# A mixer's input projection as 2x2 block products with seven multiplications

## The chip, the core and the metric

The kernel runs on one core of a Trainium2 chip. A core has a matrix engine (TensorE, "PE" in the profile; the loading of its stationary operand is listed apart as "PEld"), a vector engine (VectorE, "DVE"), an engine for functions of one argument (ScalarE, "ACT"), a general one (GpSimd, "POOL") and one that starts transfers (SyncE, "SP"). Each takes its own list of instructions in order, and they wait for each other by semaphores. [...]

The metric is the device time of one execution in microseconds: the median of three runs is 2827.87 us (2827.24 to 2828.50).

## What is computed

Three stages on 512 tokens (8 sequences of 64) of 512 numbers, all in float32: a cross attention, a state-space mixer, and a routed low-rank layer, each added to its input. The change is in the mixer:

```python
proj = einsum('bld,pd->blp', hidden_states, in_proj_w)   # hidden: the normed x
gate = proj[..., :I]                                     # I = 4096
hbc = proj[..., I:I + CONV_DIM]                          # CONV_DIM = 6144
dt = proj[..., -H:]                                      # H = 64 heads
pad = pad(hbc, ((0, 0), (K - 1, 0), (0, 0)))             # K = 4 taps
conv = conv_bias
for k in range(K):
    conv = conv + pad[:, k:k + L, :] * conv_weight[:, k]
xBC = silu(conv)                  # x (4096), B (8 x 128), C (8 x 128)
dt_p = softplus(dt + dt_bias)
dA = exp(dt_p * -exp(A_log))
# scan over tokens: state = state * dA + (dt_p * x) B^T;  y = state C
y = y + x * D
yn = (yg * rsqrt(var + EPS)).reshape(B, L, I) * norm_weight   # var per group of 512
yn = yn * silu(gate)
out = einsum('bli,di->bld', yn, out_proj_w)
```

## The kernel before, in words

The mixer (`mixer_and_routed`) works on eight groups, each of ten blocks of 128 rows of `in_proj_w`: four gate blocks (n = 0 to 3), four x blocks (4 to 7), B (8) and C (9). Its input `xnT` holds the normed tokens, transposed: 128 partitions by four chunks (`dc`) by 512 tokens.

`project(G, n)` (L1101 to L1127) makes one block: four matmuls into a PSUM bank "pj" (L1105), of which there are three, shared with the output projection "mo". A gate block is finished by one Silu on ACT (L1111). For the others DVE reads the bank four times: first tap and bias (L1116), then three taps added with a shift by one to three tokens (L1122), and ACT applies Silu (L1127).

Per 128 tokens (`tt`, four of them) there are further steps: `mix` (products of B and C, transposes of x into "px", and on DVE the tiles gm, m and dx: L1143 to L1156), `scan` (32 small matmuls into two banks, added to y by DVE: L1172, L1178), `squares` (ACT and POOL: L1184 to L1187), `gate` (DVE: y times silu(gate), L1194), `norm` (the factor rs, with Ln and Exp on ACT: L1200 to L1204) and `project_out` (L1213, added to x by DVE in L1217). `decay` makes the exponentials of the scan (matmuls L1093, Exp on ACT L1098) from tiles `av` that POOL makes (`steps`, L1078). `skip` puts x * D into y on POOL (L1134), and `load_out` scales `w_out` by the norm's weights on POOL (L1004).

The groups are pipelined by hand in the loop at L1275 and on. In the first half of a turn the new group's convolution blocks (8, 9, 4 to 7) alternate with the older group's mix, scan and gate. Then ACT changes its table from Silu to Ln and Exp, does the next group's decays and the older group's norm, and changes back; in the second half the new group's four gate blocks alternate with the older group's four output products. `tc.issue_after(ins)` keeps what its block traces on the engine of `ins` behind `ins` in that engine's list; all these uses name an instruction of ACT. Within such bounds a scheduler sets the lists when the program is built.

The first group has no older one. It is preceded by the layer norm, the dt product (`pdt`), and a chain on DVE and ACT (L1024 to L1045) that makes softplus, `dt` and `a`; from `a` come `psw` (a matmul, L1054), `ah`, `av` and the decays, behind which ACT's first Silus are put.

The block products that the change uses are in the kernel already, for the queries, keys and values of the attention: `FIRST` and `SECOND` (L38, L39) list seven products of half-size blocks, `weight_sums` (L137 to L145) makes the four sums of weights on POOL with 128x256 additions. In the queries (`project_queries`, L149 to L235) a pair's `first` step ends with sums on DVE (p1 copied by ACT at L220, then u2 at L222, t at L224), and the `second` step of the pair before runs between; banks "ab" and "cd" exist three times each.

Of the kernel before, what the change touches and what calls it, by code (L numbers as in the profile page):

```python
# [47 lines left out]
DT0 = I2 + CONV  # L48

# [901 lines left out]
def mixer_and_routed(ctx, tc, c, x, done, w_in, w_out, w_ra, b_w, out):  # L951
# [43 lines left out]
    def load_out(G):  # L995

        g = G.g
        G.wo = wst.tile([P, GC, D], F32, tag="w_out", name=f"w_out_{g}")
        nc.sync.dma_start(
            out=G.wo, in_=w_out[g * GC * P : (g + 1) * GC * P, :].rearrange("(n p) o -> p n o", p=P)  # L1000
        )
        for n in range(GC):
            ct = g * GC + n
            nc.gpsimd.tensor_scalar(G.wo[:, n, :], G.wo[:, n, :], c.nw[:, ct : ct + 1], None, op0=ALU.mult)  # L1004

    load_in(groups[0])

# [13 lines left out]

    dt = big.tile([P, NTT, H2], F32, name="dt")
    z = big.tile([P, NTT, H2], F32, name="sp_z")
    nc.vector.tensor_tensor(z, pdt, c.dtb.unsqueeze(1).to_broadcast([P, NTT, H2]), ALU.add)  # L1024
    e = big.tile([P, NTT, H2], F32, name="sp_e")
# [4 lines left out]
    u = big.tile([P, NTT, H2], F32, name="sp_u")  # L1030
    nc.vector.tensor_scalar(u, e, 1.0, None, op0=ALU.add)
    lu = big.tile([P, NTT, H2], F32, name="sp_lu")
# [68 lines left out]
    def project(G, n):  # L1101

        pj = bank("pj", [P, NT], "pj", 3)
        for dc in range(DC):
            nc.tensor.matmul(  # L1105
                pj, lhsT=G.w[:, dc, n, :], rhs=xnT[:, dc, :], start=dc == 0, stop=dc == DC - 1
            )
        if n < GC:
            if n == 0:
                G.sg = grpp.tile([P, GC, NT], F32, tag="sg", name="sg")  # L1110
            return nc.scalar.activation(G.sg[:, n, :], pj, AF.Silu).ins  # L1111
        if n == 8:
            G.xbc = grpp.tile([P, GC + 2, NT], F32, tag="xbc", name="xbc")
        ct = G.g * GC + n - GC if n < 8 else (I2 // P + G.g if n == 8 else I2 // P + G2 + G.g)
        acc = wk.tile([P, NT], F32, tag="acc", name="acc", bufs=3)
        nc.vector.tensor_scalar(  # L1116
            acc, pj, c.cw[:, ct, KC - 1 : KC], c.cb[:, ct : ct + 1], op0=ALU.mult, op1=ALU.add
        )
        accb = acc.rearrange("p (b t) -> p b t", b=B)
        pjb = pj.rearrange("p (b t) -> p b t", b=B)  # L1120
        for k in range(1, KC):
            nc.vector.scalar_tensor_tensor(  # L1122
                out=accb[:, :, k:], in0=pjb[:, :, : S - k],
                scalar=c.cw[:, ct, KC - 1 - k : KC - k], in1=accb[:, :, k:],
                op0=ALU.mult, op1=ALU.add,
            )
        return nc.scalar.activation(G.xbc[:, n - GC, :], acc, AF.Silu).ins  # L1127

    def skip(G):

        G.y = grpp.tile([P, GC, NT], F32, tag="y", name="y")
        for n in range(GC):
            ct = G.g * GC + n
            nc.gpsimd.tensor_scalar(G.y[:, n, :], G.xbc[:, n, :], c.dk[:, ct : ct + 1], None, op0=ALU.mult)  # L1134
# [99 lines left out]
    def route(tt):  # L1234
        xnT = wk.tile([P, DC, P], F32, tag="xnT", name="rt_xnT")
# [28 lines left out]
        o = wk.tile([P, D], F32, tag="o", name="o")  # L1264
# [10 lines left out]
    for g in range(G2):  # L1275
# [10 lines left out]
        with tc.issue_after(last):  # L1286

            for n, behind in (
                (None, ((mix, 0),)),
                (8, ((mix, 1),)),  # L1290
                (9, ((scan, 0),)),
                (4, ((mix, 2), (scan, 1))),
                (5, ((gate, 0), (mix, 3), (scan, 2))),
                (6, ((gate, 1), (scan, 3))),
                (7, ((gate, 2), (gate, 3))),
            ):
                if n is not None:
                    silus.append(project(G, n))
                if old:
                    for what, tt in behind:  # L1300
                        what(old, tt)
# [3 lines left out]
        with tc.issue_after(table):  # L1305
            if new:
                decay(new, 0)
                decay(new, 1)
        gates = [lambda n=n: project(G, n) for n in range(GC)]
        if new:  # L1310
# [104 lines left out]
```

## Time and profile before

| | us |
|---|---|
| median of three runs | 2827.87 |
| the profiled run | 2826.02 |
| its span, first to last instruction | 2824.3 |
| first group of the mixer, from its first projection matmul to the next group's | 2328.7 to 2372.8 (44.1) |
| one of the middle groups | 2432.1 to 2491.5 (59.4) |
| last group, to the older group's last output product | 2728.6 to 2791.1 (62.5) |

Times inside the span count from its start. A line of the table of groups of instructions names the source line, engine, operation, the written and the read tiles, shapes and count, then the busy time in us and the mean of one instruction in ns, then the idle time of the engine just before them and what ended it. A line of a timeline has the start, the duration, the engine, the source line, the operation and, in brackets, the idle time before it with what ended it. [...] A view of stretches gives the busy time of each engine in chosen parts of the span, with the granted TensorE clock (1.00 is full).

### The profile page before, as it was taken

The page shows a single profiled execution, that of the slowest core. Times are in us where ns is not written, and L with a number is a line of the kernel's source. Part 1 is how long each engine was busy: PE and PEld are TensorE (multiplying, and loading weights), DVE is VectorE, ACT ScalarE, POOL GpSimd, SP SyncE. Part 2 cuts the span into 40 slices and gives each one's busy share as a digit, 9 for nine tenths or more (in the row PEclk, how much of TensorE's full clock was granted, in tenths as well). Part 3 has the DMA queues.
Part 4 walks back from the last instruction along what each step waited for, and adds up shares of the span by engine and source line. Part 5 has one row for each costly group of instructions (what it writes and reads, how often), then busy time and mean ns, then how long its engine had stood idle before and what let it go on. Part 6 is the DMA issues. An engine that isn't in the chain of part 4 may idle for free.

```text
span 2824.3 us, 38454 instructions
## 1 busy us (share of the span) xinstructions
PE 2788.6 (99%) x14972; PEld 1980.9 (70%) x14972; DVE 1745.4 (62%) x3059; ACT 726.6 (26%) x1314; POOL 833.9 (30%) x786
## 2 busy tenths in 40 slices
PE   9899999999999999999999999999999999999998
PEld 7677777777777777777777777777777554444444
DVE  4556676676667666665666676667665416444555
ACT  3322223222222222232222222222222103222222
POOL 4323223222222332223222222322232223433431
PEclk9999999999999999999999999999999999999999
DMA  4822232232113122312311131122212441112200
GB/s 164 276 78 57 76 74 53 53 94 53 46 46 97 46 54 79 74 48 58 94 50 50 46 95 47 46 83 76 48 46 72 146 160 38 53 53 78 79 16 15
DMA packets 277230, 206.02 MB, mean 73 GB/s; under 512 B 155676, under 2 KB 240538, under 8 KB 276026
## 3 DMA queue, kind: packets, MB, share of 16 engines
q1 hardware_dynamic: 277050, 203.57, 25.2%
q8 instruction: 119, 1.95, 0.3%
q14 instruction: 61, 0.50, 0.1%
HBM read 180.87 MB, written 22.66 MB: 72 GB/s over the span
## 4 chain that ended last, share of the span: by engine, by line
PE 83%; DVE 6%; DMA 2%; ACT 1%; issue 0%; POOL 0%; SPq 0%; ACTq 0%; DVEq 0%
PE pav L596 12%; PE psc L526 11%; PE pj L1105 8%; PE pv_a L445 6%; PE pv_b L445 6%; PE pv_c L445 5%; PE pk_a L385 5%; PE pk_b L385 5%; PE pk_c L385 5%; PE mo L1213 4%; PE pv_d L445 3%; PE pk_d L385 2%; PE psn L414 2%; DMA nbs<-max_d 2%; DVE attn L574 1%; PE pvl L468 1%
## 5 line engine op out<-in xcount | busy, mean ns | idle before, releaser
L531 DVE SCALAR_TENSOR_TENSOR attn<-psc,rk,mask_sb 128x256 f32<-128x256 f32 (+1 forms) x832 | 363.4, 473 | 190.5 <-PE psc L526 188.1
L580 POOL TENSOR_TENSOR sm<-attn 128x512 f32<-128x512 f32 x64 | 82.0, 1281 | 1147.6 <-ACT attn L578 1147.6
L596 PE MATMUL pav<-attn,v 128*128 128x256 f32 (+1 forms) x1664 | 384.3, 381 | 0.0
L526 PE MATMUL psc<-q,kT 128*128 128x256 f32 x1536 | 371.5, 381 | 0.0
L596 PEld LDWEIGHTS pav<-attn,v 128*128 128x128 f32 (+1 forms) x1664 | 311.1, 190 | 55.4 <-issue 9.6
L583 POOL TENSOR_TENSOR sm<-sm,attn 128x512 f32<-128x512 f32 x256 | 339.8, 1328 | 29.4 <-DVE attn L574 10.6
L526 PEld LDWEIGHTS psc<-q,kT 128*128 128x128 f32 x1536 | 286.3, 190 | 82.4 <-issue 36.0
L1105 PE MATMUL pj<-mx_xnT,w_in 128*128 128x512 f32 x640 | 296.3, 603 | 1.3 <-DVE acc L1122 1.3
L574 DVE TENSOR_TENSOR attn<-attn,nb 128x1024 f32<-128x1024 f32 x192 | 224.7, 1216 | 68.2 <-ACT nb L571 67.9
L445 PEld LDWEIGHTS pv_a<-wv,cx 128*128 128x128 f32 x1536 | 195.5, 191 | 48.2 <-issue 41.4
L578 ACT ACTIVATE attn<-attn 128x1024 f32<-128x1024 f32 x192 | 202.5, 1058 | 71.3 <-DVE attn L574 68.5
L445 PE MATMUL pv_a<-wv,cx 128*128 128x128 f32 x1536 | 212.7, 279 | 0.0
L542 DVE TENSOR_TENSOR mx<-mx,attn 128x512 f32<-128x512 f32 x256 | 209.5, 818 | 2.0
L1105 PEld LDWEIGHTS pj<-mx_xnT,w_in 128*128 128x128 f32 x640 | 115.2, 190 | 129.4 <-issue 124.7
L385 PE MATMUL pk_a<-cx,wk 128*128 128x417 f32 (+1 forms) x512 | 193.3, 500 | 0.8 <-ACT qrs L110 0.8
L396 ACT ACTIVATE ksq<-kT 128x834 f32<-128x834 f32 (+1 forms) x128 | 109.0, 871 | 159.1 <-DVE kT L377 159.1
L637 POOL TENSOR_TENSOR o<-o,f 128x512 f32<-128x512 f32 x31 | 39.4, 1272 | 306.7 <-DMA f<-sums_d 206.3
L385 PEld LDWEIGHTS pk_a<-cx,wk 128*128 128x128 f32 x512 | 97.2, 190 | 46.1 <-issue 20.8
L1217 DVE SCALAR_TENSOR_TENSOR x<-mo,rs,x 128x512 f32<-128x512 f32 x32 | 24.0, 751 | 165.1 <-PE mo L1213 110.4
L1213 PE MATMUL mo<-w_out,y 128*128 128x512 f32 x256 | 118.1, 597 | 0.0
L571 ACT COPY nb<-nbs 128x256 f32<-128x256 f32 x64 | 24.1, 376 | 324.4 <-DMA nbs<-max_d 324.4
L1122 DVE SCALAR_TENSOR_TENSOR acc<-pj,small_consts,acc 128x504 f32<-128x504 f32 (+1 forms) x144 | 103.9, 725 | 0.7
(220 smaller groups left out, 4230.8 us busy)
## 6 DMA issues: line engine op xcount, KB each, us to landing
wk<-in_wk SPq DMA_DIRECT2D x32, 512.0 KB
wv<-in_wv SPq DMA_DIRECT2D x32, 512.0 KB
w_in<-in_w_in SPq DMA_DIRECT2D x16, 1024.0 KB
wvs<-wv_s_d SPq DMA_DIRECT2D x28, 512.0 KB
wks<-wk_s_d SPq DMA_DIRECT2D x28, 512.0 KB
cx<-in_ctxT SPq DMA_DIRECT2D x16, 834.0 KB
cx<-in_ctxT SPq DMA_DIRECT2D x16, 768.0 KB
wq<-in_wq SPq DMA_DIRECT2D x16, 512.0 KB
```

The costliest lines, as they stand in the source:

```text
L385: nc.tensor.matmul(ps[:, :w], lhsT=u.wk[l][:, dc, :], rhs=u.cx.r[ch][r][:, dc, :], start=start and dc == 0, stop=dc == 1, skip_group_check ...
L396: nc.scalar.activation(sq[ch][:, :, half, :w], u.kT[:, :, half, lo:hi], AF.Square)
L445: nc.tensor.matmul(ps[:, i * HD : (i + 1) * HD], lhsT=u.cx.r[ch][r][:, dc, i * P : (i + 1) * P], rhs=u.wv[l][:, dc, :], start=start and i ...
L526: nc.tensor.matmul(ps[:rows, t - t2, :], lhsT=lhsT, rhs=qh, start=True, stop=True)
L531: nc.vector.scalar_tensor_tensor(out=s.at[:rows, t, :].rearrange("p (h q) -> p h q", h=GQ), in0=ps[:rows, t - t2, :].rearrange("p (h q) -> ...
L542: nc.vector.tensor_tensor(s.mx2, s.mx2, s.at[:, t2 : t2 + 2, :], ALU.max)
L574: nc.vector.tensor_tensor(at[:, k : k + 4, :], at[:, k : k + 4, :], nb.unsqueeze(1).to_broadcast([P, 4, 256]), ALU.add,)
L578: nc.scalar.activation(at[:, k : k + 4, :], at[:, k : k + 4, :], AF.Exp)
L583: nc.gpsimd.tensor_tensor(sm2, sm2, at[:, i : i + 2, :], ALU.add)
L596: nc.tensor.matmul(s.av[:, 0, :], lhsT=u.v[:rows, t, hh, :], rhs=s.at[:rows, t, :], start=t == 0, stop=t == NKT - 1,)
L1105: nc.tensor.matmul(pj, lhsT=G.w[:, dc, n, :], rhs=xnT[:, dc, :], start=dc == 0, stop=dc == DC - 1)
L1213: nc.tensor.matmul(po, lhsT=G.y[:, n, tt * P : (tt + 1) * P], rhs=G.wo[:, n, :], start=n == 0, stop=n == GC - 1,)
```

## The change

1. Two blocks n and n + 1 (pairs 8 and 9, 4 and 5, 6 and 7, 0 and 1, 2 and 3: `PAIRS`) are made together. The 256 rows of weights and the 512 tokens are cut in halves, and the depth of 512 too; seven products of half size replace eight. `project` returns two steps: `first` (four products of two matmuls of 256 columns, then sums) and `second` (three products, then the rest). A pair takes two of the three "pj" banks, each holding two half results.
2. POOL makes the weight sums (`sums_in`: four 128x256 additions a pair, in three buffers), DVE four differences of blocks of xnT, once.
3. ACT copies p1 and the bank's a half, DVE adds the others into the gate tile or xbc in SBUF. The convolution then reads SBUF: the first tap with bias is on ACT, the other three on DVE as before. Silu writes in place.
4. `skip` and the scaling of w_out (`weigh_out`, now after the gate blocks) go from POOL to ACT.
5. The loop's steps are redistributed between `first` and `second`. The gate tile has one buffer instead of two, and the tiles of the softplus chain lie in a buffer of y.

```diff
-        for n in range(GC):
-            ct = g * GC + n
-            nc.gpsimd.tensor_scalar(G.wo[:, n, :], G.wo[:, n, :], c.nw[:, ct : ct + 1], None, op0=ALU.mult)
+    def weigh_out(G):
+        for n in range(GC):
+            ct = G.g * GC + n
+            nc.scalar.activation(G.wo[:, n, :], G.wo[:, n, :], AF.Copy, scale=c.nw[:, ct : ct + 1])
+
+    def sums_in(G, n):
+        l = {
+            f"L{k + 1}{e + 1}": G.w[:, 2 * e : 2 * e + 2, n + k, :] for k in range(2) for e in range(2)
+        }
+        G.l = getattr(G, "l", {})
+        G.l[n] = weight_sums(nc, l, wk.tile([P, 4, 2, P], F32, tag="ws", name="ws", bufs=3))
...
+    for o, p, q in (("T1", "R12", "R11"), ("T2", "R22", "T1"), ("T3", "R22", "R12"), ("T4", "R21", "T2")):
+        nc.vector.tensor_tensor(blocks[o], blocks[p], blocks[q], ALU.subtract)
...
     def project(G, n):
-        pj = bank("pj", [P, NT], "pj", 3)
-        for dc in range(DC):
-            nc.tensor.matmul(
-                pj, lhsT=G.w[:, dc, n, :], rhs=xnT[:, dc, :], start=dc == 0, stop=dc == DC - 1
-            )
...
+        def first():
+            st.ps = {}
+            for pair in ("ab", "cd"):
+                t = bank("pj", [P, 2, HT], f"pj_{pair}", 3)
+                st.ps[pair[0]], st.ps[pair[1]] = t[:, 0, :], t[:, 1, :]
+            for k, lhs, rhs in FIRST:
+                product(k, lhs, rhs, k in "ad", False)
+            p1 = wk.tile([P, HT], F32, tag="p1", name="p1", bufs=1)
+            nc.scalar.copy(p1, st.ps["a"])
+            st.u2 = wk.tile([P, HT], F32, tag="u2", name="u2")
+            nc.vector.tensor_tensor(st.u2, p1, st.ps["d"], ALU.add)
+            t = wk.tile([P, HT], F32, tag="t", name="t", bufs=1)
+            nc.vector.tensor_tensor(t, st.u2, st.ps["b"], ALU.add)
+            nc.vector.tensor_tensor(to[:, 1, HT:], t, st.ps["c"], ALU.add)
+
+        def second():
+            for k, lhs, rhs in SECOND:
+                product(k, lhs, rhs, False, True)
+            nc.scalar.activation(to[:, 0, :HT], st.ps["a"], AF.Silu if gate else AF.Copy)
+            nc.vector.tensor_tensor(to[:, 0, HT:], st.u2, st.ps["b"], ALU.add)
+            nc.vector.tensor_tensor(to[:, 1, :HT], st.u2, st.ps["c"], ALU.add)
+            if gate:
+                nc.scalar.activation(to[:, 0, HT:], to[:, 0, HT:], AF.Silu)
+                return nc.scalar.activation(to[:, 1, :], to[:, 1, :], AF.Silu).ins
+            for k in range(2):
+                ct = G.g * GC + n + k - GC if n < 8 else I2 // P + k * G2 + G.g
+                pj = to[:, k, :]
+                acc = wk.tile([P, NT], F32, tag="acc", name="acc", bufs=3)
+                nc.scalar.activation(
+                    acc, pj, AF.Identity, bias=c.cb[:, ct : ct + 1], scale=c.cw[:, ct, KC - 1 : KC]
+                )
+                accb = acc.rearrange("p (b t) -> p b t", b=B)
+                pjb = pj.rearrange("p (b t) -> p b t", b=B)
+                for j in range(1, KC):
+                    nc.vector.scalar_tensor_tensor(
+                        out=accb[:, :, j:], in0=pjb[:, :, : S - j],
+                        scalar=c.cw[:, ct, KC - 1 - j : KC - j], in1=accb[:, :, j:],
+                        op0=ALU.mult, op1=ALU.add,
+                    )
+                last = nc.scalar.activation(pj, acc, AF.Silu)
+            return last.ins
...
-            nc.gpsimd.tensor_scalar(G.y[:, n, :], G.xbc[:, n, :], c.dk[:, ct : ct + 1], None, op0=ALU.mult)
+            nc.scalar.activation(G.y[:, n, :], G.xbc[:, n, :], AF.Copy, scale=c.dk[:, ct : ct + 1])
...
+            for k, (n, behind) in enumerate((
+                (None, ((), ((mix, 0),))),
+                (8, (((mix, 1),), ((scan, 0),))),
+                (4, (((mix, 2), (scan, 1)), ((gate, 0), (mix, 3), (scan, 2)))),
+                (6, (((gate, 1), (scan, 3)), ((gate, 2), (gate, 3)))),
+            )):
+                steps_in = project(G, n) if n is not None else (lambda: None, lambda: None)
+                for step, also in zip(steps_in, behind):
+                    silus.append(step())
+                    if old:
+                        for what, tt in also:
+                            what(old, tt)
                 if n is not None:
+                    sums_in(G, PAIRS[k + 1])
             skip(G)
...
         with tc.issue_after(last):
+            for k, n in enumerate((0, 2)):
...
+                first, second = project(G, n)
+                first()
...
+                last_gate = second()
+                if new:
+                    sums_in(new, PAIRS[k])
...
                 if old:
-                    project_out(old, n)
+                    project_out(old, 2 * k)
+                    project_out(old, 2 * k + 1)
+            weigh_out(G)
```

## The prediction

> **What bounds the kernel now.** I read the busy shares first, then three stretches of the mixer (the first group, and the two halves of one in the middle: convolution blocks, then gate blocks with the older group's output), then the costliest groups, then timelines of the places that the change touches.
>
> ```profile
> PE 2788.6 (99%) x14972; PEld 1980.9 (70%) x14972; DVE 1745.4 (62%) x3059; ACT 726.6 (26%) x1314; POOL 833.9 (30%) x786
> ```
>
> ```profile
> 2432.10:2464.00 31.90, 31.90 (x221) 15.13 (x220) 28.28 (x49) 6.27 (x10) 18.50 (x16) 1.00 0.25 88
> 2464.00:2491.50 27.50, 27.29 (x94) 11.99 (x93) 2.87 (x4) 7.99 (x17) 4.69 (x4) 1.00 0.10 34
> 2328.70:2372.80 44.10, 42.81 (x159) 16.92 (x158) 22.83 (x41) 16.18 (x33) 18.46 (x16) 1.00 0.00 1
> ```
>
> Columns: stretch, length, then PE, weight loads, DVE, ACT, POOL busy, clock, DMA. TensorE (PE) never pauses, at full clock (1.00). But in the first half DVE is busy 28.3 of 31.9 us: it is a close second bound there, and idle in the other half. A group takes 59.4 us.
>
> ```profile
> L1105 PE MATMUL pj<-mx_xnT,w_in 128*128 128x512 f32 x640 | 296.3, 603 | 1.3 <-DVE acc L1122 1.3
> ```
>
> A float32 product is two passes, so a group's 10 x 4 products are 80 passes. The chain of waits has 8 of them in 3.43 us: 0.429 each, 34.3 us a group.
>
> **PE's share of the change.** Five pairs by seven products by two halves by two passes are 140 passes of 256 columns. The query projection has exactly these:
>
> ```profile
> 101.05 1.03 PE L204 MATMUL pq_ab<-xnT,wq 128*128 128x256 f32 x4
> 101.91 1.03 PE L204 MATMUL pq_cd<-xs,wqs 128*128 128x256 f32 x4
> ```
>
> Four start 0.86 after the last four: 0.216 each, with the 0.19 us weight loads hidden. 140 x 0.216 = 30.2, so PE is spared 4.1 us a group, 33 us in eight. That is the whole gain, if PE stays fed.
>
> **DVE's share.** A pair adds five 128x256 sums at 0.42; six blocks lose the first tap (L1116, 0.807, spacing 0.73), which goes to ACT. Per group: +25 x 0.40 - 6 x 0.73, about +5.5 us, all but 4 of it in the half where DVE is nearly full. Worse, PE now waits for DVE and ACT inside each pair. The query rows show the wait:
>
> ```profile
> 104.77 0.42 DVE L222 TENSOR_TENSOR q_u<-q_p,pq_cd 128x256 f32<-128x256 f32 x1 [3.10 <-PE pq_cd L204]
> 105.23 0.42 DVE L224 TENSOR_TENSOR q_t<-q_u,pq_ab 128x256 f32<-128x256 f32 x1
> ```
>
> u2 starts when all of `first` is done, t 0.46 later; `second` may start after t, 1.0 us after `first` ends. The queries hide this behind another pair, with six PSUM banks; the mixer has three, a pair takes two, so the next pair's c/d bank is one that this pair must vacate.
>
> **The ledger of a middle group**, from the order in which the built program issues, with durations of these rows; t = 0 is pair 8's first pass. `first` 3.46, t ready: its `second` starts at 4.5 and takes 2.6. ACT copies bank a (0.37), DVE adds b and c (done 3.1 after the start of `second`), ACT does a first tap (0.63), and DVE six taps at 0.66 (end 7.35). Only then stands u2 of the next pair in DVE's queue, and t 0.9 later: 8.3 us from `second` to `second`, against 6.05 us of PE work in a pair. The older group's m, dx, y and gate products in the same queue make it 9.4 and 9.7 by my count; PE fills with its scans, transposes, half of the next pair and an output block. From the last `second` to the last silu 8.1. So the first half takes 4.5 + 9.4 + 9.7 + 8.1 = 31.7, against 31.9: DVE has become its bound, and PE's 24 us of projections, scans and transposes, with 7 us pulled forward, don't fill it.
>
> ```profile
> 2464.05 1.28 ACT L116 ACT_TABLE_LOAD   x1
> ...
> 2465.34 0.66 ACT L1098 ACTIVATE dec<-seg 128x256 f32<-128x256 f32 x2
> ...
> 2472.18 0.20 ACT L1204 ACTIVATE rs<-rs 128x4 f32<-128x4 f32 x1
> ...
> 2472.42 0.75 DVE L1217 SCALAR_TENSOR_TENSOR x<-mo,rs,x 128x512 f32<-128x512 f32 x1 [9.05 <-ACT rs L1204]
> ```
>
> Second half: today PE bridges the 8 us from the last silu to rs with 13 us of whole blocks. After the change, ACT's queue is table load 1.28, skip 0.63, eight decays, rs (7.3 after the silu), and only then p1 of gate pair 0, which its `second` needs; behind it queue four w_out scalings (2.5 us) and the silu table, ahead of the silu that empties bank a. DVE's u2 stands behind x (0.75), so t comes 9.6 after the silu. PE has 5 to 6 us for that gap (transposes, decays, sums, half an output block): it waits 3 to 4. Then gate pair 0's `second` 2.6, three output blocks less the half done (8.6), gate pair 1 (6.05) and 0.3 of waits: 27.1, against 27.5. A group is 31.7 + 27.1 = 58.8: of 4.1 us, 0.6 is left.
>
> **POOL and the port.** POOL loses eight scalings (4 x 1.77 and 4 x 1.57 = 13.3) and gains 20 weight sums of 0.73 = 14.6: level, and each sum is issued a half group before its use, so I cost their lateness at nothing; uncovered it would be 2.9 us a pair. But the 18 taps now read two SBUF tensors (PSUM and SBUF before: 0.64 to 0.74, always). Early in the trace:
>
> ```profile
> 43.95 0.75 DVE L256 SCALAR_TENSOR_TENSOR q_st<-q_raw,qw,qrsb 128x512 f32<-128x512 f32 x1 [1.66 <-DMA qrsb<-rs_d]
> ...
> 45.71 0.72 POOL L141 TENSOR_TENSOR wqs<-wq 128x256 f32<-128x256 f32 x1 [4.42 <-DMA wq<-in_wq]
> 45.73 1.25 DVE L256 SCALAR_TENSOR_TENSOR q_st<-q_raw,qw,qrsb 128x512 f32<-128x512 f32 x1
> 46.39 1.18 POOL L143 TENSOR_TENSOR wqs<-wq 128x256 f32<-128x256 f32 x1
> ```
>
> Beside a weight sum such an op takes 1.25 instead of 0.75, and the sum 1.18 instead of 0.73: +0.5 a collision. In the order, eight or nine POOL ops fall into the three tap windows. From none to all colliding: 0 to 4.4 us; I take half, 2.2, as POOL ops also fall beside the sums from PSUM. The group is then 61.0, +1.6; six middle groups +9.6 (bounds -4 to +23).
>
> [...]
>
> **The first group** has no older work to fill with.
>
> ```profile
> 2338.68 0.41 DVE L1045 SCALAR_TENSOR_TENSOR a<-dt,a_sb 128x256 f32<-128x256 f32 x1
> ```
>
> ```profile
> 2341.29 8.05 POOL L1078 TENSOR_TENSOR av<-ah,upto 128x512 f32<-128x512 f32 x8 [53.63 <-ACT ah L1062]
> ```
>
> PE runs 26 passes of projection from 2328.7 on while the softplus chain on DVE makes `a`. In the new order PE has only pair 8's a, d and b ahead of psw, which needs `a`; ACT's p1 is queued behind all eight decays, so u2 waits for the chain, av on POOL and the decays. Without the convolutions between, but with four block differences (0.65 each), `a` comes at 2338.2, av from 2339.5 at 1.04 each, the last decay at 2345, t at 2346.3: 17.7 us after the start, in which PE has 8.8 us of work. Then three loops of 8.3 less the overlap to the last silu (24.6), and 16.2 for decays and two gate pairs: 58.5 against 43.8, +14.7. Without the 8.9 us of waits ahead of t it would be +5.8; that is my lower bound.
>
> [...]
>
> **The last group** has its sums early and much filler: 62.5 us today, PE spared 4.1, about 2 given back in waits: -2. Table loads are as many as before; in-DMAs the same; SP's order changes only in where the last loads stand. The T sums and the sp tiles are in the first group's count.
>
> **Sum.** +14.7 + 9.6 - 2 = +22 us. The profiled run took 2826.02 (span 2824.3), 1.9 under the median of 2827.87; both versions carry the same frame, so 2827.87 + 22 = 2850.
>
> **Rivals.**
> - *PE stays the bound* (faster): the waits are filled better than my ledger says. Six groups at -4.1, the last at -4, the first still +12: -17, 2811. For it: PE waited 2 us a group so far, and each pair's wait is only 1 to 3 us. Against: the loop of 8.3 is longer than a pair's 6.05. It decides if DVE's extra 2 us per pair run while PE has blocks that hold no bank. 0.15.
> - *Even groups*: no collisions, only the first group pays: -4 + 14.7 - 2 = +9, 2837. 0.2, half of it with a first group near +5.8 (a sum of 0), which is within 0.2% (5.7 us, about what can be told from none).
> - *The port* (slower still): every tap collides, and the slower taps delay each loop: 65 to 66 us a group, +6 x 6.3 + 14 = +52, 2880. 0.12.
> - *The forecast*: 2850, from 2838 to 2866. 0.53.
>
> That the change would not do what it says is excluded: the built program holds 70 products of 256 columns a group and 16 of 512.
>
> Chances: faster 0.15, same 0.1, slower 0.75. The range leaves out the far half of the first rival and of the port case: 2815 to 2875.
>
> **What would show it.** Passes of pj at 0.216 (else PE's share is wrong). Idle of PE before pj with DVE's t or ACT's p1 as releaser, 4 to 7 us a group (else the ledger). Taps with a mean of 0.75 to 0.9 (else the port). A wait of 6 us before psw in the first group, and 58 us from its first pass to the next group's. A period near 61. I am wrong if PE stays 98% busy in the middle groups.

## The result and the profile after

The changed kernel takes 2932.74 us (median of four runs, 2929.99 to 2934.11) against 2828.07 (2827.24 to 2828.50): a ratio of 1.0369, 95% interval 1.0351 to 1.0387. The forecast was +22 us with a range up to 2875; it is +105. The sign was right, the size a fifth of what came, and the time lies 58 us above the range. The profiled run took 2932.16, its span 2930.5.

From the page: busy time by engine, the granted clock in 40 slices, and the two groups of instructions that the forecast leaned on.

```profile
PE 2821.3 (96%) x15452; PEld 2108.2 (72%) x15452; DVE 1820.6 (62%) x3215; ACT 827.7 (28%) x1506; POOL 869.9 (30%) x882
...
PEclk9999999999999999999999999999999998989889
...
L1181 DVE SCALAR_TENSOR_TENSOR acc<-xbc,small_consts,acc 128x504 f32<-128x504 f32 (+2 forms) x144 | 124.9, 929 | 4.4 <-ACT acc L1175 4.4
...
L1141 PE MATMUL pj_ab<-mx_xnT,w_in 128*128 128x256 f32 x320 | 97.4, 431 | 10.2 <-DVE t L1159 6.6
```

PE has less to do (140 passes of 256 columns a group for 80 of 512) and is busy 33 us longer. Most of the reason is in the second row: from slice 34 on, in the mixer, four slices show a clock under 0.9, where the kernel before had none. The taps (L1181), 0.73 before, have a mean of 0.93 (0.96 in the middle groups). One middle group, divided at the end of its last silu, in the view of stretches (length, then PE, weight loads, DVE, ACT, POOL busy, clock, DMA):

```profile
2474.10:2513.94 39.84, 33.57 (x256) 24.81 (x254) 31.41 (x51) 14.74 (x25) 19.58 (x21) 0.96 0.18 63
2513.94:2545.37 31.43, 29.20 (x118) 18.05 (x119) 9.08 (x20) 12.12 (x25) 8.78 (x11) 0.84 0.12 40
```

The first half was 31.9 with PE never idle; it is 39.8 with 6 us of idle PE. The second was 27.5; it is 31.4 at a clock of 0.84. The 106.2 us of span that were added are: 6.0 before the first projection (2.2 of them spread over the attention, where nothing was changed; 3.6 a wait for the first weights), 22.7 in the first group (66.8 against 44.1), 75.5 in six middle groups (431.3 against 355.8), 2.0 in the last.

Where PE loses it, from the timeline of PE in the same group:

```profile
2496.98 1.03 PE L1141 MATMUL pj_ab<-mx_xs,ws 128*128 128x256 f32 x4
2501.15 0.30 PE L1216 MATMUL px<-ident,xbc 128*128 128x128 f32 x1 [3.15 <-DVE dx L1218]
2501.39 1.45 PE L1234 MATMUL py<-m,dx 64*64 64x64 f32 x32
2502.77 0.47 PE L1216 MATMUL px<-ident,xbc 128*128 128x128 f32 x1
2503.04 1.92 PE L1141 MATMUL pj_ab<-mx_xnT,w_in 128*128 128x256 f32 x4
...
2516.28 1.40 PE L1120 MATMUL seg<-av,past 64*64 64x256 f32 x8 [0.18 <-ACT dec L1125]
...
2523.84 3.78 PE L1275 MATMUL mo<-w_out,y 128*128 128x512 f32 x4 [0.18 <-DVE x L1279]
2527.41 1.76 PE L1141 MATMUL pj_ab<-mx_xnT,w_in 128*128 128x256 f32 x4
```

First a wait of 3.15 for DVE's dx. Then the same instructions take twice as long: 32 small py 1.45 instead of 0.69, four passes of pj 1.7 (start to start) instead of 0.86, later an output block 3.57 (start to start) instead of 1.72. (A listed duration runs past the next row's start: 1.03 where the next four start 0.86 later.) The reader should compare equal rows here: these rows double without an idle time of that size in brackets, and they lie in the spells in which the granted clock was 0.50, from 2501.6 to 2505.0 and from 2522.1 to 2528.9. That is the clock, not a wait.

### The profile page after: what moved, and what is told of

Its sections match the earlier page's. It is cut to its first block, busy times and chain, and to the rows that moved or that the text cites. A ratio compares the mean times of both kernels' runs of the same rounds, so it can differ in the third digit from the quotient of the medians.

```text
span 2930.5 us, 39990 instructions
## 1 busy us (share of the span) xinstructions
PE 2821.3 (96%) x15452; PEld 2108.2 (72%) x15452; DVE 1820.6 (62%) x3215; ACT 827.7 (28%) x1506; POOL 869.9 (30%) x882
## 4 chain that ended last, share of the span: by engine, by line
PE 78%; DVE 9%; DMA 2%; ACT 2%; issue 1%; POOL 0%; SPq 0%; ACTq 0%; DVEq 0%; POOLq 0%
PE pav L599 12%; PE psc L529 11%; PE pv_a L448 6%; PE pv_b L448 5%; PE pv_c L448 5%; PE pk_a L388 5%; PE pk_b L388 5%; PE pk_c L388 5%; PE pj_ab L1141 4%; DVE acc L1181 4%; PE mo L1275 3%; PE pv_d L448 3%; PE pk_d L388 2%; PE pj_cd L1141 2%; DMA nbs<-max_d 2%; PE psn L417 2%
## 5 line engine op out<-in xcount | busy, mean ns | idle before, releaser
L586 POOL TENSOR_TENSOR sm<-sm,attn 128x512 f32<-128x512 f32 x256 | 339.8, 1327 | 29.4 <-DVE attn L577 10.7
L577 DVE TENSOR_TENSOR attn<-attn,nb 128x1024 f32<-128x1024 f32 x192 | 224.7, 1215 | 68.1 <-ACT nb L574 67.6
L1275 PE MATMUL mo<-w_out,y 128*128 128x512 f32 x256 | 128.3, 641 | 1.1 <-DVE x L1279 1.1
L1181 DVE SCALAR_TENSOR_TENSOR acc<-xbc,small_consts,acc 128x504 f32<-128x504 f32 (+2 forms) x144 | 124.9, 929 | 4.4 <-ACT acc L1175 4.4
L1141 PE MATMUL pj_ab<-mx_xnT,w_in 128*128 128x256 f32 x320 | 97.4, 431 | 10.2 <-DVE t L1159 6.6
L378 ACT COPY kT<-pk_a 128x384 f32<-128x384 f32 x64 | 31.5, 493 | 266.2 <-PE pk_a L388 266.0
L422 ACT COPY kss<-psn 128x384 f32<-128x384 f32 x64 | 31.6, 494 | 250.8 <-PE psn L417 250.8
```

Source lines behind the costliest of these rows:

```text
L577: nc.vector.tensor_tensor(at[:, k : k + 4, :], at[:, k : k + 4, :], nb.unsqueeze(1).to_broadcast([P, 4, 256]), ALU.add,)
L586: nc.gpsimd.tensor_tensor(sm2, sm2, at[:, i : i + 2, :], ALU.add)
L1141: nc.tensor.matmul(st.ps[k], lhsT=l[lhs][:, dc, :], rhs=blocks[rhs][:, dc, :], start=start and dc == 0, stop=stop and dc == 1, skip_group_ ...
L1181: nc.vector.scalar_tensor_tensor(out=accb[:, :, j:], in0=pjb[:, :, : S - j], scalar=c.cw[:, ct, KC - 1 - j : KC - j], in1=accb[:, :, j:], ...
L1275: nc.tensor.matmul(po, lhsT=G.y[:, n, tt * P : (tt + 1) * P], rhs=G.wo[:, n, :], start=n == 0, stop=n == GC - 1,)
```

## The experiments

Each kernel was built from the changed one unless said otherwise. A middle group is the mean of five distances between the table loads behind the last silus. Its halves are those of one group: from pair 8's first pass to the last silu, and from there to the next pair 8. The clock is that of 2400 to 2740 us, the tap that of 2410 to 2760 us. Repeated runs of one kernel lie within 0.2% (about 5.7 us) of each other; only the kernels before, changed and those with products for the gate pairs alone were repeated, the others ran once. In no_sums_p1 the groups alternate between 58.9 and 60.5, and the halves are those of the shorter.

| kernel | us | middle group | halves | clock | mean tap |
|---|---|---|---|---|---|
| before | 2828.1 | 59.2 | 31.9 / 27.5 | 1.00 | 0.73 |
| changed | 2932.7 | 71.7 | 39.8 / 31.4 | 0.89 | 0.96 |
| no_sums | 2886.5 | 66.4 | 35.0 / 31.3 | 0.92 | 0.80 |
| psum | 2889.3 | 65.0 | | 0.96 | 0.73 |
| warm | 2912.4 | 68.2 | 39.1 / 29.8 | 0.98 | 0.98 |
| no_sums_warm | 2873.6 | 63.9 | 33.9 / 29.8 | 0.99 | |
| p1_early | 2884.3 | 64.9 | 39.0 / 26.2 | 0.95 | 0.98 |
| no_sums_p1 | 2845.2 | 59.8 | 35.1 / 23.8 | 0.98 | 0.77 |
| conv_only | 2895.8 | 67.6 | 39.9 / 27.9 | 0.95 | 1.00 |
| gate_only4 | 2813.0 | 57.5 | | 1.00 | 0.73 |

### The port: no_sums and psum

```diff
-        G.l[n] = weight_sums(nc, l, wk.tile(...))
+        G.l[n] = dict(L11=l["L11"], L12=l["L12"], L22=l["L22"], S1=l["L21"], S2=l["L11"], S3=l["L21"], S4=l["L12"])
```

> The changed kernel without the weight sums on POOL: the seven products read raw blocks of the weights in their place, so the projections are not the reference's; PE, DVE and ACT do the same work. Theory A (port, then clock): the taps that read SBUF are slowed by POOL's sums; without them they fall from a mean of 0.93 to 0.66-0.72, the two long idle stretches of PE in a middle group (3.15 us before px, the thin stretch after the last silu) get shorter by 2 to 4 us, and part of the half-clock stretches goes: a middle group of 64 to 67 us instead of 72, in all 2875 to 2900. Rival B (the chain of sums itself is longer than I counted, the port does not matter): taps stay above 0.85 or their time does not matter, 2920 to 2935. The late load of the first weights stays in both.

Measured 2886.5, a group of 66.4: theory A. Nearly all of the gain is in the first half (39.8 to 35.0), where the taps are; the second stays (31.3). The taps came to 0.80, not to 0.66 to 0.72: POOL's av and sq still meet them. What a collision looks like, in the changed kernel, first DVE's timeline, then POOL's over the same time:

```profile
2565.27 6.35 DVE L1181 SCALAR_TENSOR_TENSOR acc<-xbc,small_consts,acc 128x504 f32<-128x504 f32 x6
```

```profile
2565.63 1.17 POOL L145 TENSOR_TENSOR ws<-ws,w_in 128x256 f32<-128x256 f32 x1
2566.76 1.16 POOL L146 TENSOR_TENSOR ws<-w_in 128x256 f32<-128x256 f32 x1
2567.88 1.16 POOL L147 TENSOR_TENSOR ws<-w_in,ws 128x256 f32<-128x256 f32 x1
2568.99 1.47 POOL L1105 TENSOR_TENSOR av<-ah,upto 128x512 f32<-128x512 f32 x1
```

Six taps take 6.35 where six that meet nothing take 4.0 (4.02 in no_sums); each sum takes 1.16 instead of 0.73, av 1.47 instead of 1.04. Both engines pay.

```diff
-            nc.vector.tensor_tensor(to[:, 0, HT:], st.u2, st.ps["b"], ALU.add)
-            nc.vector.tensor_tensor(to[:, 1, :HT], st.u2, st.ps["c"], ALU.add)
+            nc.vector.tensor_tensor(st.ps["b"], st.u2, st.ps["b"], ALU.add)
+            nc.vector.tensor_tensor(st.ps["c"], st.u2, st.ps["c"], ALU.add)
...
-                pj = to[:, k, :]
+                pj = st.banks[k]
```

> The changed kernel with all its POOL sums, but DVE writes the products' sums back into the PSUM banks in place, ACT's copy of the a half is dropped, and first tap, taps and gate Silus read the banks as in the kernel before. Theory A (port): taps beside POOL's sums at 0.66-0.72 as in the kernel before, m and dx as they are; a middle group of 65 to 69 us, 2885 to 2910 in all. A's weak point is that a pair now holds both banks until its taps are read, 4 us longer, so that PE can issue less of the next pair. Rival B (chain, banks): the taps are fast but the time stays at 2920 to 2950.

Measured 2889.3, 65.0 a group. The groups of DVE's instructions, with POOL's sums all there:

```profile
L1181 DVE SCALAR_TENSOR_TENSOR acc<-pj_cd,small_consts,acc 128x504 f32<-128x504 f32 x18 | 13.2, 734 | 0.6 <-ACT acc L1175 0.2
L1181 DVE SCALAR_TENSOR_TENSOR acc<-pj_ab,small_consts,acc 128x496 f32<-128x496 f32 x18 | 13.0, 724 | 0.0
```

A tap that reads one operand from PSUM is not slowed (0.71 to 0.75 for all 108), nor is a sum (0.73), though the two do meet. Between 2410 and 2760 us 84 of 106 taps run beside a POOL instruction and take 0.73, the others 0.72. In the changed kernel 52 of 90 run beside one and take 1.13, the other 38 take 0.72. So what separates the two kernels is the tap's second SBUF operand (0.73 without it, 1.13 with it, beside POOL), not POOL's work as such. The weak point named beforehand showed too: between 2400 and 2830 us PE waited 27 us for banks that taps still held.

### The place of p1: p1_early

```diff
         with tc.issue_after(silus[-1]):
+            first0, second0 = project(G, 0)
+            first0()
             table = load_ln_exp(nc).ins
```

> The changed kernel with one change of order: in each group the first gate pair's `first` step is put ahead of the table load on ACT, so that p1 follows the last silu and no longer waits behind the skip, eight Exp of the decays and rs. Theory E (the second half is long because p1 is queued there, as my prediction had it): t comes 3 to 5 us after the last silu instead of 11, PE has `second` (2.6 us) and part of the next pair to fill the stretch, it is less empty and the clock stays up: a middle group of 64 to 68 us instead of 71.7, 2885 to 2912 in all; the first group 2 to 6 us shorter too. Rival F (the decays, rs and the output blocks behind them set the second half whatever p1 does): 2925 to 2935.

Measured 2884.3, 64.9 a group: theory E, and more than its middle. Now all of the gain is in the second half (31.4 to 26.2). ACT's queue in the changed kernel, then with early p1:

```profile
2513.94 1.28 ACT L119 ACT_TABLE_LOAD   x1
2515.24 0.72 ACT L1196 ACTIVATE y<-xbc,small_consts 128x512 f32<-128x512 f32 x1
...
2522.78 0.21 ACT L1266 ACTIVATE rs<-rs 128x4 f32<-128x4 f32 x1
2522.89 0.35 ACT L1155 COPY p<-pj_ab 128x256 f32<-128x256 f32 x1
```

```profile
2498.42 0.61 ACT L1186 ACTIVATE xbc<-acc 128x512 f32<-128x512 f32 x1
2498.94 0.35 ACT L1155 COPY p<-pj_ab 128x256 f32<-128x256 f32 x1
2499.19 0.72 ACT L1196 ACTIVATE y<-xbc,small_consts 128x512 f32<-128x512 f32 x1
2499.92 1.28 ACT L119 ACT_TABLE_LOAD   x1
```

A copy of 0.35 us stood 9 us behind work that it has nothing to do with, and a pair's whole `second` and its banks stood behind the copy. (The edit binds ACT's list alone; the scheduler may place the instructions of other engines anew, and no run tells that apart.)

### Both: no_sums_p1

The edits of no_sums and p1_early together, and the placing of the weights of p1_load (below).

> Early p1, the early load, and no weight sums on POOL (raw blocks in their place, so the projections are not the reference's): two of the three suspects taken away together. If port and p1's place explain the middle group's excess over my ledger (58.8 without collisions), a group takes 59 to 62 us, the clock stays above 0.98, and the total is 2840 to 2862. If they only hide each other (each alone gave 5 to 7 us), 63 to 65 us a group and 2865 to 2880: then something in the ledger itself is too short.

Measured 2845.2, 59.8 a group. The two savings add up: 5.3 (sums) and 6.8 (p1) alone, 11.9 together, out of 71.7. They are two separate causes, mainly one in each half of the group: beside early p1, no sums take 3.9 from the first half and 0.8 to 2.4 from the second. What stays, 17 us against the kernel before, lies in the first group: its last silu ends 19.1 us later (2378.9 against 2359.9).

### The clock: warm, no_sums_warm, p1_warm

```diff
+                if n == 0 and 0 < G.g < G2 - 1:
+                    for _ in range({"b": 6, "c": 8}.get(k, 0)):
+                        nc.tensor.matmul(st.ps[k], lhsT=zero, rhs=blocks["R11"][:, 0, :],
+                            start=False, stop=False, skip_group_check=True)
```

(4 and 10 in no_sums_warm, 8 behind "c" alone in p1_warm)

> The changed kernel plus 14 products of zero weights in each middle group (6 us of PE work that adds nothing to the bank it is accumulated in), issued behind the first gate pair's products, that is, into the two idle stretches of PE. Theory C (the clock has a price of its own): granted clock above 0.97 in the six middle groups instead of 0.83 to 0.95, the passes after the waits at 0.216 instead of 0.43, and 3 to 6 us less a group: 2897 to 2915. Rival D (the half clock falls in time in which PE waits anyway): clock up, time within 5 us of 2933, or longer by what the added products push back.

> The kernel without weight sums (raw blocks in their place, so the projections are not the reference's) plus 14 products of zero weights in each middle group, most of them behind the first gate pair's products. Without the added products a middle group took 66.4 us and the granted clock was 0.50 for about 10 us of it, from some 4 us after the last silu on, though no single wait of PE there was longer than 1 us. Theory C (the clock has a price of its own, and it is set by how full PE is over a few us, not by one long wait): clock above 0.98, the rest of the pauses stay, a middle group of 61 to 64 us, 2855 to 2872 in all. Rival D (the half clock only fills waits): 2880 to 2900, as without or longer by the added products.

> Early p1 plus 8 products of zero weights in each middle group, behind the first gate pair's products, ahead of the stretch around the last silu. With early p1 alone a middle group takes 65.0 us, and after the transposes that wait there (1.3, 0.95 and 0.8 us) the passes run at half rate for about 6 us. If the clock still costs what the doubled passes lose there, 2.0 to 2.5 us a group: 62.5 to 63.5 us, 2866 to 2874 in all. If early p1 has already taken the clock's share, 2882 to 2890 (the added 3.4 us of passes are paid in part).

Measured 2912.4 (clock 0.98, a group of 68.2), 2873.6 (0.99, 63.9) and 2884.3 (0.98, 64.8). Work that computes nothing makes the kernel faster by 20 and by 13 us: theory C, at the weak end of its range. The second of the three missed its range by 2 us. With early p1 the clock rises too (0.95 to 0.98) and the time stays, as in the second of the two forecasts: whether the added 3.4 us of passes cost what the clock wins, or the clock has no price left there, that run doesn't tell.

What the half clock costs without added work can be read inside one kernel. In no_sums_p1 the middle groups take 58.9 and 60.5 in turn. The same stretch after the last silu, in two groups one after the other:

```profile
2487.62:2500.00 12.38, 11.88 (x65) 7.25 (x66) 4.30 (x9) 8.21 (x18) 3.13 (x3) 1.00 0.00 1
2546.49:2558.90 12.41, 11.91 (x58) 6.62 (x59) 3.66 (x9) 6.64 (x15) 3.13 (x3) 0.86 0.00 0
```

PE's waits ahead of it are the same to 0.01 us (0.78, 0.79, 0.21). On PE the clock differs (1.00 against 0.86), and from last silu to the next pair 8 it is 23.8 against 25.4: 1.6 us for one spell of half clock of 3.4 us. The changed kernel has 13.7 to 17.1 us of it in a middle group.

### Which pairs: conv_only and gate_only

```diff
-            for k, n in enumerate((0, 2)):
+            for n in range(GC):
...
-                first, second = project(G, n)
-                first()
+                last_gate = block(G, n)          # project of the kernel before
```

> Products for the three convolution pairs alone; the four gate blocks are whole blocks of four matmuls as in the kernel before, interleaved with the output blocks one by one; everything else as in the changed kernel (POOL makes three pairs' sums instead of five). If the loss lies in the convolution half (port, DVE's queue, the wait before px): the second half falls to the 27.5 us of the kernel before, the first stays at about 39 less what two pairs of sums fewer on POOL spare: a middle group of 64 to 68, 2880 to 2912. If the gate pairs cost as much, 2850 to 2875. Together with the kernel that has products for the gate pairs alone (2813 in its first form), the two losses against the kernel before should add up to about 105 us if they don't feed each other.

Measured 2895.8. Second half 27.9, as in the kernel before; first half 39.9, as in the changed one. POOL makes twelve sums a group instead of twenty, but more of them meet taps: 50 of the 64 between 2410 and 2760 us. So the convolution pairs alone cost 68 us, though PE has less to do. With the 15 us that the gate pairs alone win (next run) the two add up to +53, not to the 105 of the forecast: the gate-only kernel has p1 early, which alone was worth 48, and x * D and the scaling of w_out on POOL. The other half alone is the one part of the change that pays:

```diff
+            for n, behind in ((None, ((mix, 0),)), (8, ((mix, 1),)), (9, ((scan, 0),)), ...):
+                if n is not None:
+                    silus.append(block(G, n))
+                if n in (9, 5):
+                    sums_in(G, 0 if n == 9 else 2)
...
-            nc.scalar.activation(G.y[:, n, :], G.xbc[:, n, :], AF.Copy, scale=c.dk[:, ct : ct + 1])
+            nc.gpsimd.tensor_scalar(G.y[:, n, :], G.xbc[:, n, :], c.dk[:, ct : ct + 1], None, op0=ALU.mult)
```

> Products for the two gate pairs alone, where DVE is idle: the convolution blocks, x * D and the scaling of w_out are as in the kernel before; POOL makes two pairs' sums a group, p1 of the first gate pair is put on ACT ahead of the table load, and the pool of the weights is placed so that their first load is issued early again. By PE's passes 2 x 0.81 us are spared in a group, 13 us in eight. If the second half stays filled, 2814 to 2820 (faster than before). If PE waits for t or for rs in the stretch after the last silu, 0.5 to 3 us a group are given back: 2822 to 2840.

Measured 2813.2 (ratio 0.9949, interval 0.9932 to 0.9965, against the kernel before timed beside it; so are the next three). In this form the difference T3 was written over a block that the whole convolution blocks still read, so x, B and C of the later 256 tokens come from altered data; the instructions are the same.

```diff
-    ts = big.tile([P, 3, 2, HT], F32, name="mx_xs")
-    blocks.update(T1=ts[:, 0], T2=ts[:, 1], T4=ts[:, 2], T3=blocks["R12"])
+    ts = big.tile([P, 4, 2, HT], F32, name="mx_xs")
+    blocks.update(T1=ts[:, 0], T2=ts[:, 1], T4=ts[:, 2], T3=ts[:, 3])
```

> Products for the two gate pairs alone, mended: the fourth block difference has a buffer of its own, since the whole convolution blocks still read the block that it was written over. Same instructions otherwise as the first form, which took 2813. Expected 2808 to 2820, that is 0.3 to 0.7 per cent less than before: PE is spared 13 us by its passes, and the second half stays filled. Rival: the extra 2 KB per partition move the tiles so that the first weights load late again, 3 to 5 us more.

Measured 2818.0 (0.9963; 0.9949 to 0.9976): inside, but 5 us above the first form. Its middle groups are the same (57.5); the first group is 3 us longer. PE stands in it:

```profile
2359.68 2.07 PE L1165 MATMUL pj_ab<-mx_xnT,w_in 128*128 128x256 f32 x4 [3.41 <-DVE acc L1145]
2361.54 1.91 PE L1165 MATMUL pj_cd<-mx_xs,ws 128*128 128x256 f32 x4
2363.25 1.91 PE L1165 MATMUL pj_ab<-mx_xs,ws 128*128 128x256 f32 x4
```

One wait of 3.41 us for a bank that DVE's taps hold, then twelve passes at half rate (four start 1.71 after the last four, and the clock is 0.50 from 2359.6 to 2364.9).

```diff
-                first, second = project(G, n) if k else (None, second0)
+                first, second = ((lambda: block(G, n)), (lambda: block(G, n + 1))) if not old else project(G, n) if k else (None, second0)
```

> Products for the gate pairs of groups 2 to 8 alone; the first group, where the pair waited 3.4 us for two banks and then ran at half clock for 5 us, has whole gate blocks. Against 2818 for products in all eight groups: the 3.4 us wait and the half clock go, the spared 1.6 us of the first group too: 2812 to 2817, 0.4 to 0.55 per cent less than before. Rival: the wait only moves within the first group, since its end is set by the convolution's taps on DVE: 2817 to 2820.

Measured 2820.2 (0.9973; 0.9963 to 0.9983): the rival. Whole blocks in the first group don't help: the wait of 3.41 us stands ahead of them as well, so the pair was not its cause. DVE is late there: `a` starts at 2342.9 in the form before this one, at 2339.9 in the first.

```diff
-        nc.vector.tensor_tensor(blocks[o], blocks[p], blocks[q], ALU.subtract)
+        nc.gpsimd.tensor_tensor(blocks[o], blocks[p], blocks[q], ALU.subtract)
```

> Products for the gate pairs alone, with the four block differences of the first group made by POOL instead of DVE, whose softplus chain and taps set the first group's end. 2.6 us less on DVE there: the first group from 45.1 to 42 to 43.5 us, 2813 to 2817 against 2818. Rival: POOL is late with them or slows DVE's chain by the port: 2818 to 2821.

Measured 2813.0 (2812.87 to 2816.72; ratio 0.9944, interval 0.9931 to 0.9958): with the first form the lowest time found, 0.56% less than before, and the best of those that compute the same. The first group takes 42.0 instead of 45.1, and the wait for the bank is 1.29 instead of 3.41: DVE sets the first group's end. Two middle groups in the view of stretches:

```profile
2403.99:2461.54 57.55, 57.53 (x337) 31.47 (x336) 34.55 (x62) 15.35 (x30) 28.74 (x29) 1.00 0.19 65
2461.54:2519.10 57.56, 57.56 (x338) 31.67 (x337) 34.55 (x62) 15.36 (x31) 28.36 (x29) 1.00 0.19 64
```

PE is full at full clock: here, and only here, the spared passes (2 x 0.81 a group) become time.

### Parts that moved, and two that didn't help

```diff
-            nc.scalar.activation(G.wo[:, n, :], G.wo[:, n, :], AF.Copy, scale=c.nw[:, ct : ct + 1])
+            nc.gpsimd.tensor_scalar(G.wo[:, n, :], G.wo[:, n, :], c.nw[:, ct : ct + 1], None, op0=ALU.mult)
```

(and x * D the same way)

> The changed kernel with x * D and the scaling of w_out back on POOL, as in the kernel before; the rest as changed, p1 late. Theory A (the port): 13 us more of POOL work a group beside the taps, more collisions, a middle group of 73 to 78 us, 2940 to 2970. Theory E (ACT's queue behind the last silu is what is long): rs and p1 come 0.7 us sooner and the silu behind w_out's scalings 2.5 us sooner: 69 to 71 us, 2915 to 2930.

Measured 2933.0, 70.9 a group: no difference in the total that can be told, but the trace shows parts that cancel. A middle group is 0.8 us shorter, inside theory E's range, though the taps' mean is 1.01 instead of 0.96, theory A's mechanism at a small price (18 x 0.05 = 0.9 us). In the first group POOL now has the scalings ahead of av, PE waits 7.8 us for av where it waited 1.6, and the last silu ends 9.7 us later.

```diff
-                nc.scalar.activation(acc, pj, AF.Identity, bias=c.cb[:, ct : ct + 1], scale=c.cw[:, ct, KC - 1 : KC])
+                nc.vector.tensor_scalar(acc, pj, c.cw[:, ct, KC - 1 : KC], c.cb[:, ct : ct + 1], op0=ALU.mult, op1=ALU.add)
```

> The changed kernel with the first tap and bias on DVE again, now reading xbc in SBUF. DVE gets 6 x 0.4 to 0.8 us a group in the half where it is the bound, the way through ACT (0.81 and two handovers a pair) goes. By DVE as the bound 2 to 4 us a group more: 2945 to 2960. By the chain as the bound about the same or less: 2920 to 2935.

Measured 2950.3, 75.1 a group, 3.4 more than the changed kernel, all of it in the first half (43.3 against 39.8), where DVE is busy 3.0 longer: DVE's load is what the first half goes by. Of the parts that moved, the first tap is better on ACT.

```diff
     grpp = ctx.enter_context(tc.tile_pool(name="mx_grp", bufs=2))
-    wst = ctx.enter_context(tc.tile_pool(name="mx_w", bufs=2))
     big = ctx.enter_context(tc.tile_pool(name="mx_big", bufs=1))
+    wst = ctx.enter_context(tc.tile_pool(name="mx_w", bufs=2))
```

> The kernel with p1 of the first gate pair ahead of the table load (2884 us), and the weights' pool placed behind another one in SBUF, so that the first group's weights don't lie where the attention's last tiles lie. Theory G (the load is late because it waits for PE's last reads of those tiles): the wait of 3.6 us ahead of the first projection and the 1.5 us wait for POOL's first sums go, 2878 to 2881 in all. Rival: the first group ends no sooner, since it waits for the softplus chain anyway: 2883 to 2886.

Measured 2884.9 against 2884.3: the rival. The wait for the weights goes, and PE then stands before psw:

```profile
2339.51 1.12 PE L1081 MATMUL psw<-a,ident 128*64 128x256 f32 x4 [4.22 <-DVE a L1072]
```

The edits of psum, p1_early and p1_load together:

> Early p1, the early load, POOL's sums kept, and sums, taps and Silus in the PSUM banks (in-place sums, no copy of the a half). Without early p1 this form took 65.0 us a group with 27 us of waits for banks that the taps still held and 13 us for POOL's av. If p1's place was what made the second half long, 60 to 63 us a group, 2845 to 2868. If the banks bind (pair 0 needs two banks, and pair 6 holds two until its taps are read, so p1 can't be early), no gain: 64 to 66 us, 2875 to 2890.

Measured 2882.3, 65.0 a group: the forecast of the case that the banks bind. Between 2400 and 2830 us PE waits 27.6 us for banks that taps hold, as without early p1 (26.8).

## Why the prediction was wrong

By its own steps. The second, third and fourth add up to the miss of a middle group; the clock, the first, runs through all three.

- **The clock** has no term in the sum: its price was put at nothing, and that failed. The kernel before shows a half clock in the very rows that I read for the queries, behind a wait of 2.27 (below, the line and two stretches around it). In the changed kernel the clock falls to one half three times in the middle group shown (from 2501.6, 2515.2 and 2522.1 on), 13.7 us in all. The added zero products win 3.5 us of 71.7 net of their own cost, 2.5 without the sums. In no_sums it comes with no wait of PE over 0.8 us ahead of it (last section).

```profile
86.84 1.13 PE L204 MATMUL pq_cd<-xs,wqs 128*128 128x256 f32 x4 [2.27 <-POOL wqs L142]
84.58:87.99 3.41, 1.15 (x5) 1.05 (x6) 0.00 (x0) 0.74 (x1) 2.99 (x6) 1.00 0.92 274
87.99:91.40 3.41, 3.41 (x9) 2.71 (x9) 0.05 (x1) 0.37 (x1) 2.75 (x4) 0.50 0.96 326
```

- **The second half, 27.1**, failed. "Ahead of p1 stand table load, skip, eight decays and rs" was right, and the price was not. rs ended 9.05 after the last silu, where I took 7.3. The rows of the kernel before that I had shown already say 8.3 from the start of the table load to the end of rs, at full clock and without a skip between, so the term was too short by itself. t followed 2.05 behind rs (2.3 in my count) and came 11.1 after the silu (forecast 9.6). Then an output block at half rate stood ahead of `second`, which began at 13.5, 3.9 late. Without sums the half is still 31.3, so 4.2 us are this step's; with p1 early it falls by 5.2 to 7.5.
- **The port, 2.2 us a group**, was mis-sized. "Port" is a name for what the rows show, a tap and a POOL operation that take longer beside each other; what they share, no run shows. A collision costs what the early row said (+0.44 to +0.48 measured, 0.5 taken). But I took half of eight or nine to collide, and 52 of 90 taps did, ten of the 18 in a group. The taps' mean, 0.96 against 0.73, makes 18 x 0.23 = 4.1 us, near the 4.4 that I had named as the most, and taking the sums away wins 5.3 a group, 4.8 of it in the first half. The rival "port" had the cause; its 65 to 66 us a group lie 2 to 3 above 58.8 + 4.4, and no run shows a term for them. The slowing came with two operands in SBUF: a tap beside POOL's work takes 1.13, and the taps from PSUM stay at 0.73.
- **The first half, 31.7 without collisions**: 35.0 without sums. The ledger's 9.4, 9.7 and 8.1 were some 1 us short each: in no_sums they are 10.2, 10.7 and 9.4. In the first two the six taps still meet sq and av (4.6 and 4.7 instead of 4.0); the rest of the excess has no run of its own.
- These three, 4.2 + 3.3 + (5.3 - 2.2) = 10.6, are the miss of a middle group (71.7 against 61.0). That no_sums_p1 takes 59.8, near the ledger's 58.8, is in part luck: its halves are 35.1 and 23.8, not 31.7 and 27.1.
- **The first group**, 58.5 forecast, 66.8 measured. (The 43.8 of the kernel before in that sum is 44.1 in its rows.) The mechanism was half right. The wait of 6 us before psw didn't come (0.84), since PE itself started 3.6 us late. t came late as forecast: `second` of pair 8 began 18.9 after the start (17.7). Then each loop took 9.2 instead of 8.3, and spells of half clock came on top (clock 0.85).
- **"SP's order changes only in where the last loads stand"** was wrong. With smaller pools ahead of it, the first weights' tile lies where the attention's last tiles lie, and its load waits for PE's last reads of them: 3.6 us ahead of the first projection. It proved not to be on the path (p1_load).
- Where the waits would show: I named PE before pj, with t or p1 as releaser, 4 to 7 us a group. They stand at transposes (px) that are queued ahead of pj, and what ends them is mostly dx, which stands behind the taps in DVE's queue. The view of PE's waits from 2400 to 2830 us:

```profile
PE px L1216 <- DVE dx L1218: 25.4, 16, 3.1
PE px L1216 <- ACT xbc L1186: 9.5, 14, 1.4
...
PE pj_ab L1141 <- DVE t L1159: 2.6, 5, 0.5
```

- Right: the passes at 0.216 (four in 0.86), and DVE as the bound of the first half (tap_on_dve). Wrong for a small sum: the last group, +2.0 against -2. Wrong as a reading: "PE waited 2 us a group so far", in the first rival; the rows of the two halves leave 0.2.

## What to carry to other kernels

Where PE is full, count not only the waits that a change makes but how empty each stretch of 3.4 us becomes: in these traces the clock halved behind every one in which PE was busy for less than 0.4 of it (80 of 80, 13 of 13 in the changed kernel), and the matmuls of the chain that made the stretch empty then took longer too (four passes 1.7 us instead of 0.86). Put fewer-but-dependent products where the engine that joins them is idle (here the gate half, -0.56%) and leave blocks that need nothing where it is busy. A short instruction placed behind a long queue that it doesn't depend on is worth looking for first: moving one copy of 0.35 us won 48 us.

## What the runs showed of the hardware

The half clock needs no long wait. In no_sums, after the last silu at 2492.6, no wait of PE is over 0.8 us, yet the clock halves. The stretches begin and end where the clock changes:

```profile
2492.64:2496.05 3.41, 1.96 (x15) 1.16 (x16) 1.38 (x2) 2.65 (x5) 0.01 (x1) 1.00 0.00 0
2496.05:2499.47 3.42, 2.84 (x20) 1.16 (x18) 0.00 (x0) 1.22 (x4) 2.08 (x2) 0.50 0.00 0
2499.47:2502.88 3.41, 2.84 (x20) 2.37 (x16) 0.26 (x2) 1.31 (x6) 1.04 (x1) 0.50 0.00 0
2502.88:2506.29 3.41, 3.23 (x12) 1.48 (x9) 3.08 (x8) 3.39 (x6) 0.00 (x0) 0.50 0.00 0
2506.29:2509.71 3.42, 3.42 (x15) 2.66 (x14) 0.20 (x1) 0.81 (x2) 0.00 (x0) 1.00 0.00 0
```

A stretch with PE busy for 1.96 of 3.41 us is followed by the half clock, and it stays for 10.2 us while PE is busy for 2.84 and 2.84, until a stretch with 3.23.

The 3.41 us come from the traces. All 170 spells of half clock in the 18 traces that end inside the span (20 of them in the changed kernel, one in the kernel before) last one, two, three or four times 3.41 us, as if the clock were decided anew at fixed times that far apart. I divided every trace at these times, from 20 to 2800 us. At full clock 80 stretches had PE busy for less than 0.4 of them (13 in the changed kernel, one before), and the half clock followed every one; it followed none with more than 0.84 (0.69 in the changed kernel); in between both came (the half clock behind four of 37 there). The full clock came back only behind a stretch with 0.84 or more (0.86 there). What exactly is counted stays open, since the ends of matmuls in these busy times are modelled.

So it also matters where a pause falls against these times. In no_sums_p1 the same pauses, 58.87 us apart, left PE busy for 1.63 of one such stretch, and the half clock followed. A group earlier the emptiest one had 2.10, and it did not:

```profile
2544.51:2547.92 3.41, 1.63 (x8) 0.87 (x8) 1.85 (x4) 3.39 (x6) 0.00 (x0) 1.00 0.00 0
2486.48:2489.89 3.41, 2.10 (x13) 1.32 (x17) 2.42 (x5) 3.08 (x6) 0.00 (x0) 1.00 0.01 2
```
